# Two spectral layers of a four-layer kernel: order of the last stores and reloads, zero fills on GpSimd, and products that nobody reads

## Chip, core and metric

The kernel runs on one core of one Trainium2 chip. The metric is the device time of one execution in microseconds. The core has five engines with queues of their own: TensorE (PE in the profile, its weight loads PEld), VectorE (DVE), ScalarE (ACT), GpSimd (POOL) and SyncE (SP). SP, and here also ACT, issue the DMAs.

## What is computed

Four layers follow each other on one image of 48 x 48 tokens with 768 channels: a transformer block, a spectral layer, a scan of 12 diffusion steps, and a second spectral layer with weights of its own. Only the spectral layers are touched. Cut to what matters, one of them is:

```python
def _L3_conv_ref(x, w1, b1, w2, b2):
    xs = jnp.fft.rfft2(x, axes=(1, 2))            # 48 x 25 modes, 8 blocks of 96 channels
    xs = xs.reshape(B, H, Wm, NUM_HEADS, BLOCK)
    xr, xi = jnp.real(xs), jnp.imag(xs)
    o1r = relu(einsum(xr, w1[0]) - einsum(xi, w1[1]) + b1[0])
    o1i = relu(einsum(xi, w1[0]) + einsum(xr, w1[1]) + b1[1])
    o2r = einsum(o1r, w2[0]) - einsum(o1i, w2[1]) + b2[0]
    o2i = einsum(o1i, w2[0]) + einsum(o1r, w2[1]) + b2[1]
    out_c = softshrink(o2r, LAMBDA) + 1j * softshrink(o2i, LAMBDA)
    return jnp.fft.irfft2(out_c.reshape(B, H, Wm, C), s=(H, W), axes=(1, 2)) + x
```

## The kernel before

All values are 32-bit floats. The Fourier transforms are products with constant matrices. Along the width they are done row by row, and the half spectrum goes to two arrays in DRAM, `yu[0]` and `yu[1]`, one for each half of the channels, with 50 rows (25 modes, real and imaginary). Everything along the height is done by `spectrum_mix`, which both spectral layers call: the first under the name `f1` (from `afno_first`), the second under `f3` (from `afno_second`).

**Items.** `spectrum_mix` works on items (group of channels, chunk `kc` of 5 modes, block of 96 channels). Both layers have 40 items: `f1` has 2 groups of 4 blocks, `f3` has 4 groups of 2 blocks, and each group has 5 chunks. An item goes through four stages, and step `s` of the loop issues, in this order, the stage of four different items: `s_ifft_h` of item `s-4` (one product, and an addition to the spectrum that was loaded, L1682 and L1684), `s_mlp2` of item `s-3` (ten products, L1666 and L1667, and the shrinking, L1670 and L1672), `s_mlp1` of item `s-1` (three products, L1645 to L1647, then ACT, DVE, two ReLUs on ACT at L1655 and a sign change on POOL at L1656), and `s_fft_h` of item `s` (five products, L1631, a copy by ACT at L1633, and a sum on POOL at L1635). After each step the caller's `beside(step)` runs. The first of the three products of `s_mlp1` needs the POOL sum of its item. Steps 0 to 2 have no second layer yet, and steps 40 to 43 only empty the pipeline.

**Order.** The framework schedules each engine's instructions by priority in the order of the program, but lets one that is ready go ahead. `tc.keep_in_program_order(ins)` ties an instruction behind the one that was traced last on its engine. It ties nothing behind `ins`. DMAs of SP and ACT take eight completion semaphores in turn, in the order in which they were scheduled. A DMA first waits until the DMA that had its semaphore before has landed.

**Layer `f1`.** `afno_first` first fills the unused columns (48 to 63 of each row of 64) of three tiles with zeros on POOL: `xh`, which receives half of the layer's output, and two `homes`, which receive rows of the other half during the scan (L1754 and L1755). Then `spectrum_mix` runs over 40 items. `beside` does a few other things in between, among them the last rows of the layer's own input at steps 1 and 4. The way back along the width to `xh` begins at step 40.

**Layer `f3`.** When the last block of a chunk is through, `put` (L1865) stores the chunk to `yu` from SP (L1869). For groups 0 to 2, `put` reloads all 50 rows with six DMAs into a tile `gt` after the last chunk (L1877). For the last group (`final` = 3), the stores and reloads are tied in program order on SP, and each chunk of 10 rows is reloaded by two DMAs directly after its store. The last chunk of all is stored and reloaded in two halves, one for each block. `back(group, c)` (L1883) turns a third of the width's modes of a group back with four sets of products (L1891), copies the results out of PSUM on ACT and DVE (L64 and L66), and stores them to the output. For groups 0 to 2 these are two DMAs on ACT. For the last group they are two DMAs for every half of a third, on ACT and SP in turn. `backs` (L1900) gives the steps at which groups 0 to 2 are turned back: 8, 10 and 12 steps after the end of the group. Group 3 follows after `spectrum_mix`.

**Unread products.** `keep_warm` (L127) issues `n` products whose result nobody reads. `f3` calls it once before (L1907), with 8 products of a 96 x 96 matrix with 384 columns, between the last step and the way back of group 3. A product of 32-bit floats shows as two matmuls in the profile, so these are 16.

Of the kernel before, what the change touches and what calls it, by code (L numbers as in the profile page):

```python
# [21 lines left out]
G = 48  # L22
# [4 lines left out]
NH, HD = 12, 64  # L27
# [16 lines left out]
NB, BS = 8, 96  # L44
KW = G // 2 + 1
KC = 5
# [1547 lines left out]
def spectrum_of(yu, kc, cols):  # L1594
    return yu[2 * KC * kc : 2 * KC * (kc + 1), :, cols].rearrange("(k r) p c -> (r p) k c", r=2)


def spectrum_mix(tc, name, opened, psum, side, groups, put, beside):
# [10 lines left out]
    with tc.tile_pool(name=f"{name}_s", bufs=2, side=side) as sp:  # L1609
# [80 lines left out]
        items = [(g, kc, b) for g, (_, _, n) in enumerate(groups) for kc in range(NKC) for b in range(n)]  # L1690

        stages = {s_ifft_h: 4, s_mlp2: 3, s_mlp1: 1, s_fft_h: 0}
        for step in range(len(items) + 4):
            for stage, behind in stages.items():
                if 0 <= step - behind < len(items):
                    stage(step - behind)
            beside(step)
# [42 lines left out]
def afno_first(tc, a, yu, xh, rp, follow_in, load_next):  # L1740

    nc = tc.nc
    ev = Evac(nc)
    HC = NC // 2  # L1750
    iw = rp.tile([P, 2, G], F32, tag="iw", name="f1_iw")
    homes = [rp.tile([P, HC, 8 * HD], F32, tag=f"x2{i}", name=f"x2_{i}") for i in range(2)]
    in_rows = lambda v: v.rearrange("p c (h w) -> p c h w", w=HD)
    for v in (xh, *homes):  # L1754
        nc.gpsimd.memset(in_rows(v)[:, :, :, G:], 0.0)  # L1755
    gts = {}

    def load(half, g):
        gts[half, g] = load_spectrum(nc, rp, yu, half, g, "f1", 4)

    def back(half, g, dst, psum):
        gt = gts.pop((half, g))
        for ct in range(HC):
            ps = psum(f"w_{half}_{g}_{ct}")
            rows = ps[:, :TB].rearrange("p (j b s w) -> p j s b w", j=2, b=2, s=2)
            for i in range(4):
                nc.tensor.matmul(rows[:, i // 2, i % 2], lhsT=gt[:, i, ct * P : (ct + 1) * P], rhs=iw, start=True, stop=True)
            ev(in_rows(dst)[:, ct, :, :G], ps[:, :TB].rearrange("p (h w) -> p h w", w=G))

    with (  # L1770
        tc.tile_pool(name="f1_f", bufs=1, side="right") as fp,
        tc.tile_pool(name="f1_p", bufs=8, space=PSUM) as pm,
    ):

        def psum(tag):
            return pm.tile([P, 512], F32, tag="m", name=f"f1_{tag}")

        follow = follow_in(fp, 1)

        def first_back(g):  # L1780
            back(1, g, xh[:, :, 8 * g * HD : 8 * (g + 1) * HD], psum)
            if g + 4 < NTB:
                load(1, g + 4)

        def beside(step):
            last = 2 * NKC * (NB // 2)
            if step in (1, 4):
                follow(psum)
            elif step == 8:
                nc.sync.dma_start(iw, a["iw2"])  # L1790
                load_next()
            elif last - 12 <= step < last - 4 and step % 2 == 0:
                load(1, (step - last + 12) // 2)
            elif step >= last:
                first_back(step - last)

        with ExitStack() as stack:
            groups = [(half, 0, NB // 2) for half in (1, 0)]
            opened = spectrum_open(tc, stack, "f1", a, "L1", yu, "left", groups, 3)

            def put(group, kc, us, cols):
                nc.sync.dma_start(spectrum_of(yu[groups[group][0]], kc, cols), us[:, :, cols])

# [12 lines left out]


def afno_second(tc, a, scan, yu):

    nc = tc.nc
    ev = Evac(nc)
    out = a["out"].rearrange("(p s w) c -> s w p c", s=2, w=G)
    x3, scan_psum = next(scan)
    with ExitStack() as stack:
        GB = 2
        groups = [(n * GB // (NB // 2), n * GB % (NB // 2), GB) for n in range(NB // GB)]  # L1830
        opened = spectrum_open(tc, stack, "f3", a, "L3", yu, "right", groups, 5)
# [12 lines left out]
        for n, _ in enumerate(scan):  # L1844
            if n and n % 2 == 0:
                rows_in(n // 2 - 1, scan_psum)
            if n == 4 * NTB - 1:
                rows_in(2 * NTB - 1, scan_psum)
        bp = stack.enter_context(tc.tile_pool(name="f3_b", bufs=2, side="left"))
        pm = stack.enter_context(tc.tile_pool(name="f3_p", bufs=8, space=PSUM))  # L1850

        def psum(tag):
            return pm.tile([P, 512], F32, tag="m", name=f"f3_{tag}")

        gts = {}
        W = GB * BS
        x3p = x3.rearrange("p (j b) c -> p b j c", b=2)

        def channels(group):
            half, b0, _ = groups[group]  # L1860
            return slice(half * TB + b0 * BS, half * TB + b0 * BS + W)

        final = len(groups) - 1

        def put(group, kc, us, cols):  # L1865
            half, b0, _ = groups[group]
            cs = slice(b0 * BS + cols.start, b0 * BS + cols.stop)
            pin = tc.keep_in_program_order if group == final else lambda ins: ins
            pin(nc.sync.dma_start(spectrum_of(yu[half], kc, cs), us[:, :, cols]))  # L1869
            if kc == 0:  # L1870
                gts[group] = bp.tile([P, G // 2, W], F32, tag="gt", name=f"f3_gt_{group}")
            if group == final or kc == NKC - 1:
                rows = slice(2 * KC * kc if group == final else 0, 2 * KC * (kc + 1))
                step = G // 2 if group == final else 8
                for r0 in range(0, G // 2, step):
                    for b in range(2):
                        pin(nc.sync.dma_start(gts[group][b * HD + rows.start : b * HD + rows.stop, r0 : r0 + step, cols], yu[half][rows, b * (G // 2) + r0 : b * (G // 2) + r0 + step, cs]))  # L1877

        def store(queue, prs, cols):
            for s in range(2):  # L1880
                queue.dma_start(out[s, :, prs, cols], x3[s * HD : s * HD + G, prs, cols])

        def back(group, c):  # L1883
            cols = channels(group)
            gt = gts[group].rearrange("p (j s) c -> p s j c", s=2)
            for j in range(2):
                ps = [psum(f"w_{group}_{c}_{j}_{b}") for b in range(2)]
                for b in range(2):
                    keep = slice(b * HD, b * HD + KR)
                    for s in range(2):  # L1890
                        nc.tensor.matmul(ps[b][s * HD : (s + 1) * HD, : 2 * W], lhsT=iw[keep], rhs=gt[keep, s, 4 * c + 2 * j : 4 * c + 2 * j + 2, :], start=True, stop=True)  # L1891
                for b in range(2):
                    ev(x3p[:, b, 4 * c + 2 * j : 4 * c + 2 * j + 2, cols], ps[b][: HD + G, : 2 * W].rearrange("p (j c) -> p j c", j=2))
                if group == len(groups) - 1:
                    store((nc.scalar, nc.sync)[j], slice(8 * c + 4 * j, 8 * c + 4 * j + 4), cols)
            if group < len(groups) - 1:
                store(nc.scalar, slice(8 * c, 8 * c + 8), cols)

        each = NKC * GB
        backs = {each * (q + 1) + 8 + 2 * c: (q, c) for q in range(final) for c in range(3)}  # L1900

        def beside(step):
            if step in backs:
                back(*backs[step])

        spectrum_mix(tc, "f3", opened, psum, "left", groups, put, beside)
        keep_warm(tc, psum("warm"), opened[0][0], opened[0][1][:, :2].rearrange("p n r c -> p (n r c)"), 8)  # L1907
        for c in range(3):
            back(final, c)

# [107 lines left out]
```

## Time and profile before

| | us |
|---|---|
| time, median of 3 runs (3582.03 to 3585.97) | 3582.45 |
| time of the profiled execution | 3582.01 |
| its span, first to last instruction | 3580.2 |
| PE busy in the span (98%) | 3507.9 |
| DVE busy (56%) | 2002.3 |
| ACT busy (32%) | 1140.0 |
| POOL busy (19%) | 679.5 |
| `f1`: first `s_fft_h` of 40 items | at 2609.9 |
| `f3`: first `s_fft_h` of 40 items | at 3341.3 |
| `f3`: last addition to the spectrum starts (L1684) | at 3549.4 |
| way back of group 3 starts on PE | at 3566.5 |
| last DMA issued by SP | at 3576.0 |

The rows with "at" are places in the profiled execution, counted from the start of its span. The profiled execution takes 1.8 us more than its span, and lies 0.4 us under the median. PE's busy time counts a matmul from its start to its modelled end, at whatever clock, so 98% doesn't mean that PE did its work at full speed. The granted clock over the whole span is 0.989 of full speed.

### The profile page before, as it was taken

The page shows a single profiled execution, that of the slowest core. Times are in us where ns is not written, and L with a number is a line of the kernel's source. Part 1 is how long each engine was busy: PE and PEld are TensorE (multiplying, and loading weights), DVE is VectorE, ACT ScalarE, POOL GpSimd, SP SyncE. Part 2 cuts the span into 40 slices and gives each one's busy share as a digit, 9 for nine tenths or more (in the row PEclk, how much of TensorE's full clock was granted, in tenths as well). Part 3 has the DMA queues.
Part 4 walks back from the last instruction along what each step waited for, and adds up shares of the span by engine and source line. Part 5 has one row for each costly group of instructions (what it writes and reads, how often), then busy time and mean ns, then how long its engine had stood idle before and what let it go on. Part 6 is the DMA issues. An engine that isn't in the chain of part 4 may idle for free.

```text
span 3580.2 us, 52877 instructions
## 1 busy us (share of the span) xinstructions
PE 3507.9 (98%) x21238; PEld 2149.6 (60%) x21238; DVE 2002.3 (56%) x3015; ACT 1140.0 (32%) x1735; POOL 679.5 (19%) x566
## 2 busy tenths in 40 slices
PE   9999999999999999989999999999999998999997
PEld 5666554444444444555555555555578777996685
DVE  7644467776776776564243324232245478995454
ACT  1321255555555555103101210120023265223332
POOL 3211101111111110340000000000023303981131
PEclk9999999999999999999999999999999999999999
DMA  8555556655545443343346334534544403104356
GB/s 276 201 189 190 186 155 184 181 157 148 154 124 151 124 125 87 120 157 121 108 139 175 116 108 137 158 109 127 144 122 115 110 20 105 37 28 106 97 143 132
DMA packets 282167, 480.38 MB, mean 134 GB/s; under 512 B 39206, under 2 KB 235462, under 8 KB 275704
## 3 DMA queue, kind: packets, MB, share of 16 engines
q1 hardware_dynamic: 266568, 456.13, 43.9%
q10 hardware_dynamic: 15344, 20.75, 1.9%
q8 instruction: 171, 2.80, 0.3%
q14 instruction: 84, 0.69, 0.1%
HBM read 330.82 MB, written 145.98 MB: 133 GB/s over the span
## 4 chain that ended last, share of the span: by engine, by line
PE 90%; DVE 3%; DMA 3%; POOL 2%; ACT 1%; issue 1%; SPq 0%; ACTq 0%; POOLq 0%; DVEq 0%
PE p L996 14%; PE p L1059 13%; PE s L657 12%; PE av L688 12%; PE qk L375 6%; PE c L1223 4%; PE s L667 3%; PE c L1323 3%; PE v L180 3%; PE pj L180 2%; PE f_z L1666 2%; PE f_z L1667 2%; PE f_x L1631 2%; PE so L1410 2%; PE f_u L1682 2%; PE f_o L1645 1%
## 5 line engine op out<-in xcount | busy, mean ns | idle before, releaser
L677 DVE TENSOR_TENSOR acc<-acc,p 128x928 f32<-128x928 f32 (+1 forms) x480 | 561.1, 1169 | 258.8 <-ACT p L669 217.6
L669 ACT ACTIVATE p<-s 128x928 f32<-128x928 f32 (+1 forms) x540 | 505.9, 939 | 488.1 <-PE s L667 468.6
L657 PE MATMUL s<-qt,kv 64*128 64x464 f32 (+1 forms) x2160 | 520.8, 558 | 5.7 <-DMA qt<-q_d 5.7
L1059 PE MATMUL p<-w,h 128*128 128x384 f32 x1512 | 492.3, 487 | 0.0
L688 PE MATMUL av<-p,kv 128*64 128x464 f32 (+1 forms) x2160 | 442.6, 554 | 0.0
L1059 PEld LDWEIGHTS p<-w,h 128*128 128x128 f32 x1512 | 285.7, 190 | 198.8 <-issue 4.2
L667 PE MATMUL s<-bt,oneh 64*128 64x464 f32 (+1 forms) x1080 | 399.8, 729 | 0.8 <-DMA bt<-rh_d 0.8
L688 PEld LDWEIGHTS av<-p,kv 128*64 128x64 f32 x2160 | 147.0, 137 | 261.2 <-issue 248.8
L657 PEld LDWEIGHTS s<-qt,kv 64*128 64x128 f32 x2160 | 203.2, 187 | 162.0 <-issue 153.6
L996 PE MATMUL p<-x2nT,w 128*128 128x384 f32 x864 | 292.8, 489 | 4.2 <-POOL rr L1035 4.2
L1323 PE MATMUL c<-H,bands 128*48 128x96 f32 x5632 | 244.6, 247 | 10.9 <-DVE th L1261 8.3
L375 PE MATMUL qk<-xnT,wqk 128*128 128x384 f32 x756 | 249.8, 487 | 0.1
L1323 PEld LDWEIGHTS c<-H,bands 128*48 128x48 f32 x5632 | 234.8, 123 | 20.9 <-issue 8.7
L996 PEld LDWEIGHTS p<-x2nT,w 128*128 128x128 f32 x864 | 164.8, 191 | 120.8 <-POOL rr L1035 4.4
L996 PE MATMUL p<-xT,w 128*128 128x384 f32 x648 | 220.8, 486 | 0.0
L1035 POOL TENSOR_TENSOR rr<-rr,ml_b 128x1152 f32<-128x1152 f32 x12 | 31.8, 2649 | 944.7 <-DMA rr<-xr_d 828.3
L991 ACT ACTIVATE h<-h,ml_b 128x384 f32<-128x384 f32 x144 | 88.3, 614 | 345.8 <-DVE h L1011 173.6
L375 PEld LDWEIGHTS qk<-xnT,wqk 128*128 128x128 f32 x756 | 141.5, 190 | 93.1 <-issue 0.7
L1331 POOL TENSOR_TENSOR t<-s,c 128x768 f32<-128x768 f32 x80 | 144.4, 1828 | 180.8 <-DVE s L1294 168.2
L996 PEld LDWEIGHTS p<-xT,w 128*128 128x128 f32 x648 | 123.2, 190 | 85.8
L667 PEld LDWEIGHTS s<-bt,oneh 64*128 64x128 f32 x1080 | 106.8, 187 | 105.4 <-issue 103.3
L1666 PE MATMUL f_z<-f_w,f_o 97*96 97x96 f32 x800 | 134.2, 249 | 0.0
(334 smaller groups left out, 4594.0 us busy)
## 6 DMA issues: line engine op xcount, KB each, us to landing
w<-w1s_d SPq DMA_DIRECT2D x36, 768.0 KB
w<-w2s_d SPq DMA_DIRECT2D x36, 768.0 KB
w<-w1s_d SPq DMA_DIRECT2D x36, 576.0 KB
w<-in_mlp_w_dram SPq DMA_DIRECT2D x27, 768.0 KB
yu<-f_ys SPq DMA_DIRECT2D x48, 384.0 KB
wqk<-wqk_d SPq DMA_DIRECT2D x12, 1344.0 KB
bt<-rw_d SPq DMA_DIRECT2D x72, 174.0 KB
bt<-rh_d SPq DMA_DIRECT2D x72, 174.0 KB
```

Of the source, the lines that this page charges most:

```text
L180: nc.tensor.matmul(p[:, :TB], lhsT=rhs[n][:, c, t * P : (t + 1) * P], rhs=w[:, c, :], start=c == 0, stop=c == NC2 - 1)
L375: nc.tensor.matmul(p[:, :TB], lhsT=w[:, n, c, :], rhs=ops[sb][n][:, c, :], start=c == 0, stop=c == NC2 - 1)
L657: nc.tensor.matmul(ps[:, s, :n], lhsT=keys[pr % 2][rows, kt * P : (kt + 1) * P], rhs=held(c)[rows, :n], start=True, stop=False)
L667: nc.tensor.matmul(ps[:, s, :n], lhsT=oneh[rows, b % 2, :], rhs=bts[b // 2][rows, j, :n], start=False, stop=True)
L669: nc.scalar.activation(p, ps[:, :, :n], AF.Exp)
L677: nc.vector.tensor_tensor(probs[c], probs[c], p, ALU.add)
L688: nc.tensor.matmul(avs[c][rows, : size(c)], lhsT=vals[pr % 2][:, kt, rows], rhs=p[:, s, :], start=kt == 0, stop=kt == NT - 1)
L996: nc.tensor.matmul(p[:, :TB], lhsT=w[n][:, c, :], rhs=rhs[n][:, c, :], start=c == 0, stop=c == NC2 - 1)
L1059: nc.tensor.matmul(ps[t][:, :TB], lhsT=hs[left, f][:, t * P : (t + 1) * P], rhs=wt[:, f % KW2, :], start=f == 0, stop=f == NF2 - 1)
L1323: nc.tensor.matmul(ps[r0 : r0 + G, k // 4, cols], lhsT=bands[:, n - GC, i, :] if gr else bands0[:, n, i, :], rhs=H[:, n, :, d : d + NPR], ...
L1331: GP.tensor_tensor(t, sc[:, ch], c1[:, m0 : m0 + GC].unsqueeze(2).to_broadcast([P, GC, RR, NPR]), ALU.mult)
L1666: nc.tensor.matmul(out, lhsT=o1[:, j, 1:3, :].rearrange("c r h -> c (r h)"), rhs=w2t[:, b, 0, :], start=True, stop=False)
```

## The change

`spectrum_mix` gets seven unread products: three before step 0, two at the start of step 1 and two at the start of step 2. They use a PSUM tile of their own, the first that the loop takes. Both layers get them.

In `f1` the three zero fills at the start are gone. Nine smaller ones, each for a third of a tile (one of three channel tiles), are issued at the end of steps 9 to 17, each tied behind what POOL was given before it.

In `f3` the last chunk is stored as a whole. The chunk before it (`kc` 3) is stored without its reload, so that the order on SP is: store of chunk 3, store of chunk 4, two reloads of chunk 3, the first reload of chunk 4. The second reload of chunk 4 is issued by ACT. The three parts of the way back of group 2 are issued at steps 38, 39 and 40, where they were at 38, 40 and 42. The unread products at the end become 12, from 8.

```diff
         stages = {s_ifft_h: 4, s_mlp2: 3, s_mlp1: 1, s_fft_h: 0}
+        warm = psum("first")
+        unread = lambda n: keep_warm(tc, warm, fh, w1t[:, :2].rearrange("p n r c -> p (n r c)"), n)
+        unread(3)
         for step in range(len(items) + 4):
+            if 0 < step < 3:
+                unread(2)
             for stage, behind in stages.items():
...
-    for v in (xh, *homes):
-        nc.gpsimd.memset(in_rows(v)[:, :, :, G:], 0.0)
+    edges = [in_rows(v)[:, ct, :, G:] for v in (xh, *homes) for ct in range(HC)]
...
         def beside(step):
             last = 2 * NKC * (NB // 2)
+            if 8 < step < 9 + len(edges):
+                tc.keep_in_program_order(nc.gpsimd.memset(edges[step - 9], 0.0))
...
         def put(group, kc, us, cols):
             half, b0, _ = groups[group]
-            cs = slice(b0 * BS + cols.start, b0 * BS + cols.stop)
+            if cols.stop < W:
+                return
+            cs = slice(b0 * BS, b0 * BS + W)
             pin = tc.keep_in_program_order if group == final else lambda ins: ins
-            pin(nc.sync.dma_start(spectrum_of(yu[half], kc, cs), us[:, :, cols]))
+            pin(nc.sync.dma_start(spectrum_of(yu[half], kc, cs), us))
             if kc == 0:
                 gts[group] = bp.tile([P, G // 2, W], F32, tag="gt", name=f"f3_gt_{group}")
-            if group == final or kc == NKC - 1:
-                rows = slice(2 * KC * kc if group == final else 0, 2 * KC * (kc + 1))
-                step = G // 2 if group == final else 8
-                for r0 in range(0, G // 2, step):
+
+            def reload(queue, b, rows, r0, n):
+                pin(queue.dma_start(gts[group][b * HD + rows.start : b * HD + rows.stop, r0 : r0 + n], yu[half][rows, b * (G // 2) + r0 : b * (G // 2) + r0 + n, cs]))
+
+            chunk = lambda k: slice(2 * KC * k, 2 * KC * (k + 1))
+            if group < final and kc == NKC - 1:
+                for r0 in range(0, G // 2, 8):
                     for b in range(2):
-                        pin(nc.sync.dma_start(gts[group][...], yu[half][rows, ..., cs]))
+                        reload(nc.sync, b, slice(0, KR), r0, 8)
+            elif group == final and kc != NKC - 2:
+                for k in (kc,) if kc < NKC - 1 else (kc - 1, kc):
+                    for b in range(2):
+                        reload(nc.scalar if k == NKC - 1 and b else nc.sync, b, chunk(k), 0, G // 2)
...
-        backs = {each * (q + 1) + 8 + 2 * c: (q, c) for q in range(final) for c in range(3)}
+        backs = {each * (q + 1) + 8 + (2 if q < final - 1 else 1) * c: (q, c) for q in range(final) for c in range(3)}
...
-        keep_warm(tc, psum("warm"), opened[0][0], opened[0][1][:, :2].rearrange("p n r c -> p (n r c)"), 8)
+        keep_warm(tc, psum("warm"), opened[0][0], opened[0][1][:, :2].rearrange("p n r c -> p (n r c)"), 12)
```

More of the change, by code (lines that the diff above doesn't have):

```diff
@@ L1866, in put @@
             half, b0, _ = groups[group]
-            cs = slice(b0 * BS + cols.start, b0 * BS + cols.stop)
+            if cols.stop < W:
+                return
+            cs = slice(b0 * BS, b0 * BS + W)
             pin = tc.keep_in_program_order if group == final else lambda ins: ins
-            pin(nc.sync.dma_start(spectrum_of(yu[half], kc, cs), us[:, :, cols]))
+            pin(nc.sync.dma_start(spectrum_of(yu[half], kc, cs), us))
             if kc == 0:
                 gts[group] = bp.tile([P, G // 2, W], F32, tag="gt", name=f"f3_gt_{group}")
-            if group == final or kc == NKC - 1:
-                rows = slice(2 * KC * kc if group == final else 0, 2 * KC * (kc + 1))
-                step = G // 2 if group == final else 8
-                for r0 in range(0, G // 2, step):
-                    for b in range(2):
-                        pin(nc.sync.dma_start(gts[group][b * HD + rows.start : b * HD + rows.stop, r0 : r0 + step, cols], yu[half][rows, b * (G // 2) + r0 : b * (G // 2) + r0 + step, cs]))
+            def reload(queue, b, rows, r0, n):
[3 more added lines that the diff above has]
+                for r0 in range(0, G // 2, 8):
+                    for b in range(2):
+                        reload(nc.sync, b, slice(0, KR), r0, 8)
[3 more added lines that the diff above has]
+                        reload(nc.scalar if k == NKC - 1 and b else nc.sync, b, chunk(k), 0, G // 2)
         def store(queue, prs, cols):
```

## The prediction

> **What bounds the kernel now.** The page gives PE 98% busy and 90% of the chain of waits, so the question is where PE works slowly or stands still in the two spectral layers. I cut the stretches that the change touches out of the busy times by window (columns: length, busy time and instructions of each engine, granted PE clock, DMA share, GB/s):
>
> ```profile
> 2609.90:2626.90 17.00, 11.36 (x61) 9.58 (x62) 3.25 (x9) 4.13 (x9) 6.33 (x8) 0.60 0.99 271
> 3341.20:3356.40 15.20, 12.25 (x62) 10.48 (x63) 2.60 (x7) 4.13 (x9) 3.63 (x5) 0.55 0.21 52
> 3356.40:3370.00 13.60, 13.60 (x115) 11.45 (x114) 7.86 (x15) 5.03 (x12) 4.39 (x6) 1.00 0.21 55
> 3548.00:3566.50 18.50, 6.27 (x22) 2.86 (x19) 2.08 (x5) 0.48 (x1) 0.00 (x0) 0.75 0.59 112
> ```
>
> The first two rows are the first items of `f1` and `f3`: PE has gaps and only 0.55 to 0.60 of its clock. The third row is the running pipeline, PE full at full clock. The fourth is the end of `f3`, where little runs.
>
> The timeline shows the POOL part of the first stretch:
>
> ```profile
> 2616.72 0.81 POOL L1656 TENSOR_SCALAR f_o<-f_o 96x240 f32<-96x240 f32 x1 [4.34 <-ACT f_o L1655]
> 2617.48 2.01 POOL L1755 MEMSET xh<- 128x2304 f32 x1
> 2619.43 0.78 POOL L1755 MEMSET x<- 128x384 f32 x2
> 2620.18 0.69 POOL L1635 TENSOR_TENSOR f_Xs<-f_X 96x240 f32<-96x240 f32 x1
> 2620.92 0.39 PEld L1645 LDWEIGHTS f_o<-f_Xs,f_w 96*96 96x96 f32 x2 [4.41 <-POOL f_Xs L1635]
> ```
>
> The fills stand between the sign change of item 0 and the sum of item 1, whose copy had ended at 2617.34. PE waits 4.41 us for that sum.
>
> The SP part of the timeline, for the end of `f3`:
>
> ```profile
> 3547.45 0.31 SPq L1869 DMA_DIRECT2D yu<-f_us  x1
> 3550.40 1.24 SPq L1877 DMA_DIRECT2D f_gt<-yu  x2
> 3552.82 0.45 SPq L1869 DMA_DIRECT2D yu<-f_us  x1
> 3558.19 0.69 SPq L1877 DMA_DIRECT2D f_gt<-yu  x2
> 3558.98 0.31 SPq L1869 DMA_DIRECT2D yu<-f_us  x1
> 3563.11 0.69 SPq L1877 DMA_DIRECT2D f_gt<-yu  x2
> 3566.53 6.68 PE L1891 MATMUL f_w<-f_gt,iw 50*64 50x384 f32 x48 [12.19 <-DMA f_gt<-yu]
> ```
>
> Store and reload take turns: chunk 3, then the two halves of chunk 4. Each reload waits for its store to land, and the next store stands behind it on SP. The last data exist at 3550.08 (second L1684 at 3549.43, 0.65 us), and PE starts at 3566.53. Finally SP's waits:
>
> ```profile
> SPq L1869 <- DMA out_dram<-x: 9.4, 3, 6.3
> ```
>
> Stores to `yu` also wait for output DMAs of `back` of group 2 (issued by ACT at 3540.73 and 3549.02), which had their semaphores before them.
>
> **What the Trainium skill says.** (1) "TensorE: Matmul & The Clock Gate", Part 1: PE's clock falls to half after an idle window of about 3.4 us and comes back after a busy one; the window runs freely. The trace agrees: after gaps of 1.8 and 1.5 us the pair of L1646 takes 1.01 us (2613.34) where it takes 0.57 at full clock (3356.87), and full speed is back some 13 us later. (2) "DMA: Bandwidth & Descriptors", "Two DMAs through the same engine are not ordered": a DMA that reads what another wrote must wait for that one's completion. That is the 2.95 us (3547.45 to 3550.40) to 5.4 us of each store above. (3) Same page, "Issuing engines are not separate DMA queues": a second issuing engine only saves issue time. Two reloads on SP take 0.69 us, so ACT saves about 0.35.
>
> **The change, part by part.** The profiled execution took 3582.0 us (span 3580.2), 0.4 under the median.
>
> *First items, pace.* From one item's first-layer weight load to the next's, before: `f3` 3343.78, 3349.52, 3356.38, that is 5.7 and 6.9 us; `f1` 2612.43, 2620.92, 2626.91, that is 8.5 and 6.0. At full clock, from the load at 3356.38 the next item's sum ends at 3360.82; with 0.06 for PE to react the shortest pace is 4.5. The steady pace is 4.57.
>
> *Do the unread products hold the clock?* A call is two matmuls at a spacing of 0.323 us (3549.02 to 3549.34 and on), so 0.645. Two calls, 1.29, fill the gap of 1.45 before the first `s_mlp1` (PE gap at 2612.44 and 3343.78); in step 2 they leave about 1 us of the gap idle. I take it that the clock stays at 1.00. Then both layers need 2.51 (first `s_fft_h` to first `s_mlp1`, as before) + 4.5 + 4.5 = 11.5 us to the third `s_mlp1`, after which PE is full.
>
> *The three at the start.* In `f3`, PE starts at 3341.27, just after DVE had emptied the last PSUM tile of the scan at 3341.17. The unread tile is now the first of its pool and I take it to wait for the same, so 3 x 0.645 = 1.9 us come on top. In `f1` PE is free at 2608.07, the last PSUM tile is emptied at 2608.67 (2606.82 + 1.85), and the spectrum lands for PE's start at 2609.9. So three calls end at 2610.65: +0.8. If they wait for PE alone the cost is nothing (gains 0.8 and, in `f3`, 1.8 more); at half clock it is twice.
>
> *Fills.* They cost 2.0 and 0.42 us for 2304 and 384 columns, which makes 0.10 + 0.83 ns per column: a third costs 0.74 or 0.2. In a running step POOL is idle 3.1 us after its sum (its wait before L1656 at full pace), and the tie puts each fill there. Zero; were it before the sum instead, at most 3 x 0.74.
>
> *Sum of both starts.* `f1`: before 2626.91 - 2609.89 = 17.0; after 0.8 + 11.5; gain 4.7. `f3`: before 3356.38 - 3341.24 = 15.1; after 1.9 + 11.5; gain 1.7. Behind `f1` everything waits for its results, so the gain passes through.
>
> *Way back of group 2 moved.* It takes 1.52 us of PE (16 matmuls). Step 39 and step 40 are full, step 42 waits for DVE. One part leaves step 42, where it cost little, and comes into step 39: the last addition ends at 3551.3 instead of 3550.1 (+1.4 for PE, -0.2 as DVE copies less before it). In return all four output DMAs are issued by about 3542.5 and land (6.7 us at worst, 3540.73 to 3547.45) before the last store: the waits for semaphores vanish.
>
> *Last chunk.* Store 3 goes out when its data are there, about 3543.5. Store 4 follows at 3551.4 with nothing before it. Landing: 2.95 as for store 3, which is as large; 3.2 taken, up to 5.4 beside other traffic. Reloads of chunk 3 are issued meanwhile. Reloads of chunk 4 go out at 3554.6. They took 3.4 until PE started (3563.11 to 3566.53), for half the width; twice the bytes, 0.35 less issue: 3.7 (3.1 to 4.6). PE starts at 3558.3: gain 8.2. The reload on ACT waits for store 4; behind it on ACT stand only the copies of group 3, which need it anyway.
>
> *End.* 12 unread calls from 3550.3 take 7.74 us, to 3558.0, just before PE is wanted; if the reload is faster they delay it, by 0.3 at most. PE then starts at full clock: 48 matmuls in 4.6 (3 x 1.52) and not 6.68. The first output DMA left 2.9 us after PE's start and would leave 1.2 earlier; the DMA rate at the end (up to 275 GB/s for 1.77 MB) limits the rest. Gain 2.0 (0.5 to 3).
>
> Sum: 4.7 + 1.7 + 8.2 + 2.0 = 16.6 us. 3582.0 - 16.6 = 3565.4; with the 0.4 of the median, 3565.9.
>
> **Rivals.** About 0.2%, 7 us, is what a measurement can tell from no change.
> - *The clock falls anyway.* Unread calls at half clock take 2.6 instead of 1.29 and delay the items: `f1` -2.7 (fills) + 0.8 + 1.1 + 1.2 = +0.4, `f3` 1.9 + 1.1 + 1.2 = +4.2, end -8.2: 3.6 less, 3578.8. For it: windows with a 1.5 us gap lost the clock before. Against: the gaps are mostly filled now.
> - *The end pays less.* Store 4 takes 5.4, reloads 4.6, and the outputs stay bound by DMA: the end gives 4.9 in place of 10.2; 3571.2.
> - *A gain of `f1` is lost in the scan*, whose loads of bands and angles stand in the chain with 9.71 and 7.85 us: if they end no earlier, 3570.6. Against: their room is freed only after `f1`.
> - *Slower.* The four output DMAs of steps 39 and 40 now follow each other on ACT. If each of three had to wait for a semaphore whose DMA had just gone out, at 6.6 us (3540.73 to 3547.4), ACT would hold the last two items' ReLUs back 19.8 us: 3582.4 - 16.6 + 19.8 = 3585.6. It decides from 16.6 us on. Against: before, ACT's output pairs went out in 0.85 to 0.92 us, and its waits for semaphores ahead of them were 1.3 us at most.
>
> **Numbers.** Forecast 0.60; end pays less 0.15; lost in the scan 0.12; clock falls 0.09; slower 0.04. Faster by over 0.2%: 0.87; within: 0.09; slower: 0.04. The lower end of the range takes starts without PSUM waits (-2.6) and an end better by 1.9 (the lower bounds above); the upper end takes in both cases around 3571, with 4 us more for their coming partly together, and leaves out the last two: 3561 to 3575.
>
> **What would show it.** Right: clock near 1.00 in the first 12 us of both layers; pace 4.5 from item 0 on; no fill between sign change and sum; store 4 under 0.2 us after the last addition; PE's way back starting 7 us after that addition ends, where it was 16.4; its 48 matmuls in under 5 us. Wrong: a clock near 0.6 with the unread matmuls spaced 0.64; a store that waits for an output DMA; ACT standing still in steps 40 to 42.

## The result, and where the time went

| | before | changed |
|---|---|---|
| time, median of 17 runs each, us | 3585.97 | 3575.55 |
| lowest and highest | 3580.32, 3588.72 | 3573.19, 3579.94 |
| profiled execution: time, span | 3582.0, 3580.2 | 3578.7, 3576.8 |

The ratio is 0.9976, with a 95% interval of 0.9969 to 0.9982: by it the change gains 8.6 us (6.5 to 11), where 16.6 had been forecast; the medians themselves differ by 10.4. The forecast's 3565.9 was counted from the first three runs of the kernel before (3582.45), its range ended at 3575, and the changed kernel's median is 3575.55. The direction was right, the size was not.

The two profiled executions can't be compared by their spans. PE ends the MLP ahead of `f1`, before any changed instruction, at 2608.07 before and at 2614.49 in the changed kernel. In the twelve experiments, whose instructions up to there are the changed kernel's, that place lies between 2606.91 and 2613.80, so it scatters by itself. I therefore cut both executions at the same places of the program and compare the stretches:

| stretch, us | before | changed | gain | forecast |
|---|---|---|---|---|
| end of the MLP to the third first-layer load of `f1` (PEld L1645) | 18.84 | 14.22 | 4.6 | 4.7 |
| from there to `f3`'s first work on PE (rest of `f1`, scan) | 714.36 | 712.53 | 1.8 | 0 |
| from there to the third first-layer load of `f3` | 15.11 | 13.42 | 1.7 | 1.7 |
| from there to the first part of group 2's way back | 171.97 | 171.96 | 0.0 | 0 |
| from there to the end of the last addition | 21.73 | 24.75 | -3.0 | -1.2 |
| from there to the start of group 3's way back | 16.45 | 11.88 | 4.6 | 9.4 |
| from there to the end of the span | 13.67 | 13.55 | 0.1 | 2.0 |
| sum | 972.1 | 962.3 | 9.8 | 16.6 |

Both starts came out as forecast, and the three last rows did not. The busy times by window of the changed kernel (columns: length, busy time and instructions of PE, PEld, DVE, ACT, POOL, granted clock, DMA share, GB/s), for the first items of `f1` and of `f3`, and for the time between the last addition and the way back:

```profile
2617.20:2628.70 11.50, 9.93 (x71) 7.34 (x69) 2.79 (x8) 3.92 (x9) 3.62 (x5) 1.00 1.05 259
3343.20:3354.70 11.50, 9.97 (x72) 7.38 (x70) 1.91 (x5) 3.92 (x9) 3.62 (x5) 1.00 0.19 51
3551.40:3563.20 11.80, 7.02 (x22) 3.26 (x20) 0.00 (x0) 0.00 (x0) 0.00 (x0) 0.93 0.62 94
```

The clock of the first items is 1.00 where it was 0.60 and 0.55, and both take the 11.5 us that the forecast's steps gave. The timeline of `f1` shows the sum right behind the sign change, with no fill between them, and a load 4.5 us after the one before (2619.69):

```profile
2622.72 0.81 POOL L1656 TENSOR_SCALAR f_o<-f_o 96x240 f32<-96x240 f32 x1 [3.08 <-ACT f_o L1655]
2623.49 0.69 POOL L1635 TENSOR_TENSOR f_Xs<-f_X 96x240 f32<-96x240 f32 x1
2624.23 0.24 PEld L1645 LDWEIGHTS f_o<-f_Xs,f_w 96*96 96x96 f32 x2 [1.59 <-POOL f_Xs L1635]
```

The end of `f3` in the timeline of the changed kernel (start, duration, engine, line; PE, DVE and the two queues that issue DMAs):

```profile
3543.88 1.25 PE L1682 MATMUL f_u<-f_Z,f_ih 96*96 96x480 f32 x2 [1.53 <-DVE f_Z L1672]
3544.92 0.53 PE L1666 MATMUL f_z<-f_w,f_o 97*96 97x96 f32 x2
3545.24 0.53 PE L1667 MATMUL f_z<-f_w,f_o 97*96 97x96 f32 x2
...
3550.72 0.65 DVE L1684 TENSOR_TENSOR f_us<-f_u,f_yt 96x480 f32<-96x480 f32 x1 [0.58 <-PE f_u L1682]
3551.40 0.31 SPq L1877 DMA_DIRECT2D yu<-f_us  x1
3551.80 3.59 SPq L1882 DMA_DIRECT2D f_gt<-yu  x3
3555.17 0.56 ACTq L1882 DMA_DIRECT2D f_gt<-yu  x1
3563.25 6.98 PE L1906 MATMUL f_w<-f_gt,iw 50*64 50x384 f32 x48 [4.83 <-DMA f_gt<-yu]
```

Store 4 leaves SP 0.03 us after the last addition (3550.72 + 0.65 = 3551.37): the queue is free, as forecast. The two reloads of chunk 3 follow it at once, and those of chunk 4 go out 3.7 us later, when it has landed (the row of three on SP holds both of chunk 3 and the first of chunk 4, the row on ACT the second). That is also near the forecast. But PE then waits until 3563.25, 8.1 us after the issue of chunk 4's reload, where 3.7 had been forecast. In addition the ten products of the last item (L1666, L1667) run at a spacing of 0.32 us between the lines, half the pace of 0.17 at full clock, and so does the way back at the end: 6.98 us for its 48 matmuls, not 4.6.

What the DMAs did meanwhile is seen in two windows of the same kernel, first the wait for group 3's reloads, then the reloads of group 0, whose pieces are as long (192 numbers, 768 bytes) but which take 50 rows at once:

```profile
3555.00:3562.00 7.00, 3.42 (x11) 1.47 (x9) 0.00 (x0) 0.00 (x0) 0.00 (x0) 0.97 0.72 81
3405.00:3409.00 4.00, 4.00 (x34) 3.28 (x33) 2.62 (x5) 1.68 (x4) 1.08 (x2) 1.00 0.69 183
```

The last column is the point: 81 GB/s against 183, at about the same share of busy time of the DMA engines. 7 us at 81 GB/s are 567 KB, which is what was left of the 737 KB of the reloads of chunks 3 and 4 when store 4 had landed.

### The profile page after: what moved, and what is told of

The parts are those of the page before. It is cut to its first block, busy times and chain, and to the rows that moved or that the text cites. A ratio compares the mean times of both kernels' runs of the same rounds, so it can differ in the third digit from the quotient of the medians.

```text
span 3576.8 us, 52953 instructions
## 1 busy us (share of the span) xinstructions
PE 3513.7 (98%) x21274; PEld 2148.0 (60%) x21274; DVE 2004.7 (56%) x3015; ACT 1141.4 (32%) x1735; POOL 680.8 (19%) x572
## 4 chain that ended last, share of the span: by engine, by line
PE 91%; DVE 3%; POOL 2%; DMA 2%; ACT 1%; issue 1%; SPq 0%; ACTq 0%; DVEq 0%; POOLq 0%
PE p L996 14%; PE p L1059 13%; PE s L657 12%; PE av L688 12%; PE qk L375 6%; PE c L1223 4%; PE s L667 3%; PE c L1323 3%; PE v L180 3%; PE pj L180 3%; PE f_u L1682 2%; PE f_z L1666 2%; PE f_z L1667 2%; PE so L1410 2%; PE f_x L1631 2%; POOL t L1331 1%
## 5 line engine op out<-in xcount | busy, mean ns | idle before, releaser
L1666 PE MATMUL f_z<-f_w,f_o 97*96 97x96 f32 x800 | 134.1, 249 | 0.0
```

Source lines behind the costliest of these rows:

```text
L1666: nc.tensor.matmul(out, lhsT=o1[:, j, 1:3, :].rearrange("c r h -> c (r h)"), rhs=w2t[:, b, 0, :], start=True, stop=False)
```

## The experiments

One execution of a kernel scatters by several us, so the single times below decide nothing. The stretches do. Columns: (a) end of the MLP to the third first-layer load of `f1`, (b) `f3`'s first work on PE to its third such load, (c) first part of group 2's way back to the end of the last addition, (d) from there to the start of group 3's way back, (e) its 48 matmuls, (f) its start to the end of the span.

| kernel | a | b | c | d | e | f | one time |
|---|---|---|---|---|---|---|---|
| before | 18.84 | 15.11 | 21.73 | 16.45 | 6.68 | 13.67 | 3582.01 |
| changed | 14.22 | 13.42 | 24.75 | 11.88 | 6.98 | 13.55 | 3578.66 |
| e1_reload3_first | 14.22 | 14.66 | 23.14 | 12.89 | 6.68 | 13.60 | 3574.19 |
| e2_one_queue | 14.22 | 15.07 | 25.03 | 11.11 | 5.52 | 13.72 | 3578.86 |
| e3_backs_apart | 14.21 | 14.91 | 23.37 | 12.75 | 7.82 | 13.54 | 3573.77 |
| e4_warm_19 | 14.22 | 14.70 | 23.14 | 11.50 | 4.72 | 12.77 | 3576.48 |
| e5_no_first_unread | 16.33 | 15.07 | 24.94 | 11.67 | 4.98 | 13.54 | 3576.93 |
| e6_fills_at_start | 16.21 | 15.08 | 25.25 | 12.02 | 6.69 | 13.40 | 3574.85 |
| e7_gap_filled | 14.21 | 15.08 | 23.14 | 12.21 | 7.84 | 13.25 | 3570.96 |
| e8_all_three | 14.21 | 13.41 | 23.14 | 13.93 | 6.85 | 13.30 | 3575.23 |
| e9_long_pieces | 14.21 | 14.66 | 23.14 | 10.40 | 8.32 | 14.65 | 3576.86 |
| e10_twenty_rows | 14.22 | 14.72 | 23.14 | 8.31 | 4.52 | 13.01 | 3571.99 |
| e11_thirds | 14.22 | 14.88 | 23.14 | 11.54 | 6.00 | 11.83 | 3571.01 |
| e12_rows_and_gap | 14.21 | 14.74 | 23.14 | 8.65 | 6.28 | 12.48 | 3569.30 |

All edits are to the changed kernel.

### The two starts: fills and unread products

`e5_no_first_unread` takes the seven unread products and their tile away:

```diff
-        unread(3)
...
-            if 0 < step < 3:
-                unread(2)
```

> The changed kernel without the seven unread products at the first items of both layers. Theory (they hold the clock): without them the clock is 0.6 again in the first 15 us; from the end of the last matmul of the layer before to the third item's first-layer weight load, f1 takes 16.2 us (18.8 before, less 2.7 for the fills; 14.2 with the change), and f3 15.1 from its first matmul (13.5 with the change). Rival (in f1 the fills alone were it): f1 14.2 to 14.7.

`e6_fills_at_start` puts the fills back:

```diff
+    for v in (xh, *homes):
+        nc.gpsimd.memset(in_rows(v)[:, :, :, G:], 0.0)
...
-            if 8 < step < 9 + len(edges):
-                tc.keep_in_program_order(nc.gpsimd.memset(edges[step - 9], 0.0))
```

> The changed kernel with the three zero fills at the start of f1 again. Theory: they stand between the sign change of item 0 and the sum of item 1 and cost about 2.7 us, 16.9 us from the last matmul before f1 to the third item's first-layer weight load (14.2 with the change). With a longer gap the clock may fall too: up to 18. Rival (POOL has room for them beside the unread products): 14.2 to 14.5.

The first three first-layer products of `f1` in the timeline, first of `e5_no_first_unread`, then of `e6_fills_at_start`:

```profile
2615.72 1.11 PE L1645 MATMUL f_o<-f_Xs,f_w 96*96 96x240 f32 x2 [1.45 <-POOL f_Xs L1635]
2621.52 1.12 PE L1645 MATMUL f_o<-f_Xs,f_w 96*96 96x240 f32 x2 [1.48 <-POOL f_Xs L1635]
2627.30 0.61 PE L1645 MATMUL f_o<-f_Xs,f_w 96*96 96x240 f32 x2
```

```profile
2613.55 0.65 PE L1645 MATMUL f_o<-f_Xs,f_w 96*96 96x240 f32 x2 [0.16 <-POOL f_Xs L1635]
2619.03 0.92 PE L1645 MATMUL f_o<-f_Xs,f_w 96*96 96x240 f32 x2 [1.88 <-POOL f_Xs L1635]
2624.57 0.65 PE L1645 MATMUL f_o<-f_Xs,f_w 96*96 96x240 f32 x2
```

Without the unread products the pair takes 1.11 us (half clock) and the pace is 5.8. With them, but with the fills, the pair starts at 0.65 and the second waits 1.88 us for a sum that the fills delay. Alone, the moved fills gain 2.5 us (18.84 to 16.33) and the unread products 2.6; together 4.6. The clock of the first 14.1 us is 0.64 in e5, near the 0.6 expected; e6 came out 0.7 us better than expected. The forecast's steps for `f1` hold, and its gain is the same 14.2 in every kernel that has both. It isn't lost later: measured from the end of the MLP, the first product of the way back to `xh` starts at 191.5 us before and at 186.6 in the changed kernel.

`f3` is another matter. Twelve kernels have the unread products there, and only the changed kernel and `e8_all_three` show the gain of 1.7 us. The other ten lie between 14.66 and 15.08, against 15.07 to 15.11 without them. The three calls of the start, in the changed kernel and then in `e7_gap_filled`, where nothing differs up to there:

```profile
3341.24 2.15 PE L133 MATMUL f_first<-f_w,f_fh 96*96 96x384 f32 x6 [1.78 <-issue]
```

```profile
3333.56 3.50 PE L133 MATMUL f_first<-f_w,f_fh 96*96 96x384 f32 x6 [1.78 <-issue]
```

PE has stood idle for 1.78 us in both. The calls come behind this wait and can't fill it. In one kernel the clock holds, in the other it has fallen, and the calls that should keep it cost 1.4 us more. The forecast's 1.7 was met by this profile's luck; what the luck is made of is told below, with the last item. The median of the twelve is 14.7, a gain of 0.4.

### The last item: the clock and the moved way back

`e3_backs_apart` puts group 2's parts back to steps 38, 40 and 42; `e7_gap_filled` fills PE's gaps in the last two steps:

```diff
-... (2 if q < final - 1 else 1) * c: (q, c) ...
+... 2 * c: (q, c) ...
```

> The changed kernel with the way back of group 2 at steps 38, 40 and 42 again. Theory (the moved parts delay the last items, by PE time and by a fallen clock): from PE's start of the first part of group 2's way back to the end of the last addition 21.7 us, as in the kernel before, where the changed kernel has 24.7; clock 1.00 there. Against it stands what the move was to save: then the outputs of step 42 meet the last store, and from the last addition to PE's way back it takes 12.5 to 16 us instead of 11.9. Rival (nothing but the outputs matters): 24.7 us stay.

```diff
             if 0 < step < 3:
                 unread(2)
+            if name == "f3" and step > len(items) + 1:
+                keep_warm(tc, psum(f"late_{step}"), fh, w1t[:, :2].rearrange("p n r c -> p (n r c)"), 2)
```

> The changed kernel with two unread products ahead of each of the last two items' products of s_ifft_h in f3 (steps 42 and 43), where PE waits 1.4 to 1.5 us for DVE. Theory (the clock falls in that gap and the ten products of the last item's second layer take 3.3 instead of 1.7 us): from PE's first part of group 2's way back to the end of the last addition 23.1 us instead of 24.7. Rival (the moved parts cost this time by themselves): 24.4 to 25.

Column c answers. With the way back moved it is 23.14 wherever the clock held, which is the forecast's own number (21.73 + 1.4, where 1.2 had been taken). It is 24.75 to 25.25 where the clock fell in the last item. Without the filled gaps it fell in four of nine (changed, e2, e5, e6) and held in five (e1, e4, e9, e10, e11). With them it held in all three (e7, e8, e12), as the busy times of e7 from c's start to its end say (clock in the third column from the end):

```profile
3520.60:3543.80 23.20, 22.83 (x172) 14.48 (x172) 12.98 (x24) 6.55 (x16) 3.77 (x5) 1.00 0.70 147
```

Which of the two happens goes by where PE's wait falls. In all fourteen traces the granted clock changes only at places that lie multiples of 3.413 us apart: in the changed kernel at 3544.52, 3547.94, 3561.59, 3568.42 and 3571.83, which is 1, 4, 2 and 1 times that. The series lies elsewhere in each execution. In the last items PE waits once for 1.53 us (3542.35 to 3543.88 in the changed kernel) and once for 1.43. In the four executions whose clock fell, the wait of 1.53 us lies whole between two neighbouring places of the series, and the clock falls at the second; in the five where it held, one of the places lies inside it. The changed kernel, first between the places around its wait and then up to the next one:

```profile
3541.11:3544.52 3.41, 1.88 (x17) 1.48 (x16) 1.54 (x3) 0.00 (x0) 0.74 (x1) 1.00 0.89 132
3544.52:3547.93 3.41, 3.41 (x20) 3.01 (x19) 0.00 (x0) 0.00 (x0) 0.00 (x0) 0.50 0.91 215
```

In `e10_twenty_rows` the wait is from 3541.47 to 3543.00, a place of its series is at 3541.91, and the clock is held from there on:

```profile
3541.93:3545.33 3.40, 2.33 (x20) 1.88 (x21) 0.89 (x2) 0.00 (x0) 0.00 (x0) 1.00 0.97 195
```

With the calls of e7 there is no such wait, as PE isn't idle for 0.3 us at a time in this stretch, and so three out of three is more than luck. The start of `f3` goes by the same series. In the changed kernel and in `e8_all_three` a place lies inside the wait of 1.79 us and leaves 1.52 and 1.36 us of it behind; in the twelve other executions, that of before and e5 among them, 1.64 us or more lie between two places, and the clock fell in each.

In `e3_backs_apart` the clock fell too, from 3538.11 to 3541.53: one product took 1.73 us instead of 1.05, most of the ten products behind it ran at half pace, and c became 23.37 rather than 21.7. Its d is 12.75, since store 4 now shares the queues with the last output DMAs and takes 5.7 us. At full clock it would have needed 21.7 + 12.75 = 34.5 us for c and d, and the changed kernel 23.14 + 11.88 = 35.0. So moving the way back gains nothing that these runs can show.

### The reloads

`e2_one_queue` issues the last reload from SP:

```diff
-reload(nc.scalar if k == NKC - 1 and b else nc.sync, b, chunk(k), 0, G // 2)
+reload(nc.sync, b, chunk(k), 0, G // 2)
```

> The changed kernel with all reloads issued by SP. Backlog theory: the queue doesn't matter but for 0.35 us of issue, 11.9 to 12.3 us from the last addition's end to PE's way back. Rival (two queues get in each other's way): below 11 us.

PE began after 11.1 us, but with four matmuls only. It then waited for the second half of the data, with the next ones at 3564.81, which is 12.5 us after the addition. So the second queue isn't dear, and not worth much: 0.6 us (12.5 against 11.9).

My first theory for the 8.1 us was that chunk 3's reload stands ahead of chunk 4's. `e1_reload3_first` sends it before store 4:

```diff
-            elif group == final and kc != NKC - 2:
-                for k in (kc,) if kc < NKC - 1 else (kc - 1, kc):
+            elif group == final:
+                for k in (kc,):
```

> The changed kernel with chunk 3 reloaded directly after its store again, so ahead of the store of chunk 4; the rest as changed. Changed kernel: 11.9 us from the end of the last addition to PE's way back of group 3. Backlog theory (reloads move at some 80 GB/s, and after the store 737 KB of four reloads stand in line): only 368 KB are left, so 0.1 + 3.6 (store) + 4.6 (368 KB at 80 GB/s) + 1.2 (landing to PE) = 9.5 us. Rival (the reload of chunk 4 is slow by its width or by its two queues, whatever stands before it): 11.5 to 12 us.

It became worse, 12.89. SP's queue in the timeline of that kernel:

```profile
3537.55 0.31 SPq L1877 DMA_DIRECT2D yu<-f_us  x1
3545.60 0.69 SPq L1882 DMA_DIRECT2D f_gt<-yu  x2
3546.39 0.31 SPq L1877 DMA_DIRECT2D yu<-f_us  x1
3553.25 0.27 SPq L1882 DMA_DIRECT2D f_gt<-yu  x1
```

Store 3 needed 8.05 us until its reload could go: the DMA engines were full there, at shares of 1.00 to 1.12 from 3539 to 3543, with the outputs of group 2 under way. Store 4 was then ready at 3545.91 and left at 3546.39, side by side with the reload, and took 6.9 us where it takes 3.7 in the changed kernel. And with nothing else left, chunk 4's reload alone still took 5.5 us from issue to PE. So the order is not the cause. The theory fell, and the question became why ten rows take so long.

`e9_long_pieces` gives group 3 a DRAM array of its own, `e10_twenty_rows` reloads both chunks at once, `e11_thirds` cuts each reload in three:

```diff
+    yu.append(dram.tile([HD, G, 2 * BS], F32, tag="yz", name="yz"))
...
-            cs = slice(b0 * BS, b0 * BS + W)
+            cs = slice(0, W) if group == final else slice(b0 * BS, b0 * BS + W)
+            half = 2 if group == final else half
```

> Group 3's spectrum goes through a DRAM array of its own, [rows, 48, 192], so that a row of a reload is one run of 18432 bytes; in the changed kernel it is 24 pieces of 768 bytes that lie 1536 bytes apart. Bytes, queues and order are as in the changed kernel. There, 551 KB that were left of the reloads when store 4 had landed moved at 58 to 98 GB/s and took 7 us, and the way back began 11.9 us after the last addition. Theory 1, the 768-byte pieces set that rate: long pieces move at 160 GB/s or more, as the reloads of groups 0 to 2 do (162 to 210 GB/s at 3405 to 3409), the 551 KB take 3.5 us, and the way back begins 8.4 us after the last addition (8 to 9). Rival, the ten rows (ten partitions) of a reload set it: the rate stays near 80 GB/s and the 11.9 stay, within 0.5.

```diff
-                for k in (kc,) if kc < NKC - 1 else (kc - 1, kc):
-                    for b in range(2):
-                        reload(nc.scalar if k == NKC - 1 and b else nc.sync, b, chunk(k), 0, G // 2)
+                rows = chunk(kc) if kc < NKC - 1 else slice(2 * KC * (kc - 1), 2 * KC * (kc + 1))
+                for b in range(2):
+                    reload(nc.scalar if kc == NKC - 1 and b else nc.sync, b, rows, 0, G // 2)
```

> The reloads of chunks 3 and 4 are one: two DMAs of twenty rows, both behind store 4, in place of four of ten rows, two of them ahead of its landing. Pieces stay at 768 bytes, the bytes are the same. Theory 1, the pieces set the rate of 80 GB/s: 737 KB start only at about 3.1 us after the last addition, and need 9 us: the way back begins 13 us after the last addition (12.5 to 14). Rival, the rows set it (groups 0 to 2 reload fifty rows at once, in pieces of 768 bytes, at 162 to 210 GB/s): twice the rate with twenty rows, 4.6 us for the bytes and 1.3 until the first and after the last: 9.0 us (8.5 to 10).

```diff
-                        reload(..., b, chunk(k), 0, G // 2)
+                        for r0 in range(0, G // 2, 8):
+                            reload(..., b, chunk(k), r0, 8)
```

> Each reload of ten rows is cut into three of 8 pieces a row, as the reloads of groups 0 to 2 are cut: 12 DMAs in place of 4, same bytes, same pieces, same order and queues. Theory 1 (pieces) and the rival (rows) expect the rate of 80 GB/s and a way back 11.9 us after the last addition, up to 1 us later for six more issues on SP of 0.3 us. A third theory, that the rate is set by how many DMAs are under way at once (groups 0 to 2 have six): 120 GB/s or more, and a way back 10 us after the last addition or less.

Windows of four us that hold the reload behind the landing of store 4, first of `e1_reload3_first` (ten rows in pieces of 768 bytes, one DMA on SP and one on ACT), then of `e9_long_pieces` (ten rows in runs of 18432 bytes), then of `e10_twenty_rows` (twenty rows in pieces of 768 bytes, one DMA on SP and one on ACT):

```profile
3554.00:3558.00 4.00, 0.00 (x0) 0.00 (x0) 0.00 (x0) 0.00 (x0) 0.00 (x0) 0.80 0.53 92
```

```profile
3555.00:3559.00 4.00, 2.00 (x7) 0.72 (x5) 0.00 (x0) 0.00 (x0) 0.00 (x0) 1.00 0.69 92
```

```profile
3553.00:3557.00 4.00, 2.94 (x10) 1.18 (x8) 0.00 (x0) 0.00 (x0) 0.00 (x0) 1.00 0.56 181
```

With long pieces chunk 4's reload moves no faster. The 92 GB/s of its window say too much, because a packet is counted where it starts, and these packets of 18432 bytes take 2.2 us each: from the first start to the last end the reload took 5.4 us, 68 GB/s, where that of e1 took 4.1 us, 91 GB/s. d was 10.40 all the same, 1.5 us less than in the changed kernel and between the two expectations, which is not explained. But the clock then fell and f grew, so d and f together are only 0.4 us shorter (25.05 against 25.43). Twice the rows in as many DMAs (e10) move twice the bytes in the same time, 4.1 us from the first start to the last end. In thirds (e11) the rate was 82 GB/s from 3549 to 3557. So the pieces' length and the number of DMAs under way are not what limits, and the rows per DMA are. The timeline of `e10_twenty_rows`:

```profile
3548.91 0.31 SPq L1877 DMA_DIRECT2D yu<-f_us  x1
3551.88 0.28 SPq L1882 DMA_DIRECT2D f_gt<-yu  x1
3551.89 0.60 ACTq L1882 DMA_DIRECT2D f_gt<-yu  x1
3557.19 4.52 PE L1906 MATMUL f_w<-f_gt,iw 50*64 50x384 f32 x48 [1.25 <-DMA f_gt<-yu]
```

The store lands in 2.97 us with nothing beside it, the reload takes 5.3, and PE starts 8.3 us after the last addition, although no reload runs beside the store any more. It starts at full clock, because the 12 calls now end only 1.25 us ahead of it.

Why the rows count stays open. The Trainium skill ("DMA: Bandwidth & Descriptors", "Why a DMA increments its semaphore by 16 and not by 1") says that such a copy is split over the largest number of engines up to 16 that divides the slowest dimension of both sides. That is ten for ten rows and for twenty alike. The packets on record agree: each of these DMAs ends with ten packets of 4 bytes, in e1 as in e10. So the number of engines doesn't tell the two apart. What differs is the time of one packet of 768 bytes, in the mean 60 and 80 ns on the two queues with ten rows, 41 and 37 with twenty. A limit that lies with the rows, as each goes to one partition of SBUF, would fit: 92 GB/s over twenty rows under way and 181 over forty are both about 4.6 GB/s. The 78 GB/s of e2 (3556 to 3563), with all reloads on one queue, don't fit this simplest form, and no run tried such a limit by itself.

### The end

`e4_warm_19` issues 19 unread calls at the end in place of 12, so that they reach PE's start:

> The changed kernel with 19 unread products at the end instead of 12, so that they reach to within 0.5 us of the reload's landing. Theory (the clock had fallen by the way back): its 48 matmuls take 4.6 us instead of 6.98, and from their start to the end of the span 11.5 us instead of 13.6. Rival (the end is bound by the issue and landing of the output DMAs): the matmuls take 4.6, the end moves by less than 0.5 us, 13.1 or more.

The clock held and the 48 matmuls took 4.72 us, but the end came only 0.8 us nearer: 12.77, between the two expectations. The busy times from the first output DMA's issue until the data have flowed, in the changed kernel and then in `e4_warm_19`:

```profile
3566.20:3575.00 8.80, 4.02 (x34) 1.62 (x26) 2.79 (x5) 2.20 (x5) 0.00 (x0) 0.69 0.79 200
```

```profile
3564.10:3573.00 8.90, 2.55 (x28) 1.06 (x20) 2.79 (x5) 2.10 (x5) 0.00 (x0) 0.88 0.80 198
```

The outputs' 1.77 MB take the same time at 200 GB/s. A faster PE only lets the first of them go earlier, 2.2 us after its start rather than 2.9, and that difference is the gain. Column f says the same over all kernels: with 4.5 to 5.0 us for the matmuls it is 12.8 to 13.5, with 6.0 and more 11.8 to 14.7.

### Together

`e8_all_three` joined e1, e7 and 15 calls at the end, on the strength of the first theory:

> Three edits at once on the changed kernel: chunk 3 reloaded ahead of the last store, unread products ahead of the last two items' s_ifft_h, 15 unread products at the end. If each does what its theory says: 23.1 us to the last addition, 9.5 us from there to PE's way back (the 15 calls end at 9.7, so about 9.8), 4.6 us for its matmuls and 11.5 to 12 from its start to the end of the span; f3 ends 1.6 + 2.1 + 1.8 = 5.5 us earlier than with the change. If the output DMAs bind the end, 3.7.

c is the 23.14 expected, but d is 13.93: store 4 left 1.6 us after the last addition, behind chunk 3's reload, and landed 6.9 us later. It shows the cost of e1's order a second time. `e12_rows_and_gap` joins the edits of e10 and e7 instead and was timed:

> The edits of e10_twenty_rows (one reload of twenty rows for chunks 3 and 4) and of e7_gap_filled (two unread calls in each of the last two steps) together. If the rows set the rate of the reloads and the unread calls keep the clock in the last item: from the first part of group 2's way back to the last addition 23.1 us (in the changed kernel 24.75), from there to the way back of group 3 8.3 us (8 to 9; changed 11.9), 48 matmuls in 4.5 us, start to end of the span 13.0. That is 5.7 us less than the changed kernel's profile, or 3570 by its median: 0.9958 of the kernel before (0.9950 to 0.9966). Rival, what the end gains is lost in the output DMAs, which cannot move faster: start to end of the span 15 us or more, ratio 0.9970 or more.

Its median of 5 runs is 3570.63 (3567.97 to 3571.89) beside 3584.16 for 9 runs of the kernel before; the ratio is 0.9959, with an interval of 0.9945 to 0.9973. c is 23.14 and d 8.65. The median lies 5 us under that of the changed kernel (3575.55), close to the 5.7 that the stretches gave. The two intervals overlap, so the order of these two kernels rests on the stretches more than on the times. The clock fell again, 1.4 us after the start of the way back (6.28 for the matmuls), and f was 12.48 all the same.

## Why the forecast was wrong, by its steps

**Right.** *First items, pace; the fills; the three at the start of `f1`*: 14.22 us where 18.84 - 4.7 = 14.1 was forecast, with clock 1.00 and pace 4.5, and each half of it confirmed alone (e5, e6). *Behind `f1` the gain passes through*: it does. *Store 4 with nothing before it* left after 0.03 us. *No wait of a store for an output DMA*, and no stall of ACT in steps 40 to 42. *Way back of group 2 moved*: the cost of 1.2 was 1.4 at full clock.

**Wrong: the term "twice the bytes, 0.35 less issue: 3.7" of the last chunk.** It measured 8.1. The row used was for half the width, 3.4 us for 184 KB a half, and the step took the time as nearly independent of the bytes. The window that the forecast itself drew (3548.0 to 3566.5) had only a mean rate. Cut into small windows, the same trace shows the half-width reload moving at 92 GB/s:

```profile
3564.00:3566.00 2.00, 0.00 (x0) 0.00 (x0) 0.00 (x0) 0.00 (x0) 0.00 (x0) 0.50 0.52 92
```

With that, 3.4 plus 184 KB at 92 GB/s (2.0 us) is 5.4 for chunk 4, which is what e1 measured (5.5). The rest is the reload of chunk 3, "issued meanwhile": it was issued, but at this rate it needs 4 us itself and was less than half done when store 4 landed (567 of 737 KB were left). Both together are the 4.4 us. This step alone costs more than half of the missing 8.

**Wrong: "PE then starts at full clock" and the 2.0 at its end.** The calls ended at 3558.4, 4.8 us ahead of the late reload, and the clock fell: 6.98 us, gain 0.1. Had it held, e4 shows that it pays 0.8, because the output DMAs set the rest. The lower bound of 0.5 was nearer than the value taken.

**Wrong by chance: the clock in the last item, -1.6.** I had taken full clock there. It held in five of nine executions without filled gaps and fell in this one, as its wait of 1.53 us lay whole between two places of the series. The forecast had no term for this, although it had seen the clock fall after gaps of 1.8 and 1.5 us itself.

**Met by chance.** `f3`'s start paid its 1.7 here, but typically pays 0.4. The 1.8 of the scan isn't the change's either: with the same instructions, the stretch from `f1`'s third load to `f3` is 710.7 to 714.5 us over the experiments. In the trace of before the clock fell early in the scan (0.76 of full speed from 2823 to 2830), and in the changed kernel it held at the same place. But it fell there in five experiments too, with stretches of 711.8 to 714.5 us, and held in seven, with 710.7 to 712.7, so that this is a part of the scatter at most.

Of the rivals, "the end pays less" names what happened, for a reason of its own: it had 5.4 for the store and 4.6 for the reload, and it was 3.7 and 8.1. (Its 4.9 us for the end come to 5.1 with the 3.2 and 3.7 that the forecast had taken.) "The clock falls anyway" was right for the last item, the end and mostly for `f3`, and wrong for `f1`. Put in order, what the change is worth by the stretches, without the luck, is 4.6 in `f1`, 0.4 in `f3`, -1.4 to -3.0 in the last item, 4.6 in the wait and 0.1 at the end: 6.7 to 8.3, beside the measured 8.6.

## What to carry to other kernels

When a transfer stands alone on the path, read its rate in a window of a few us around it, and scale by bytes and by rows; a mean over a stage with other traffic says nothing, and a time from issue to landing hides which part grows. Before a transfer is sent earlier, ask what it then runs beside: chunk 3's reload sent ahead of store 4 made the store twice as long, and one reload of twenty rows behind it was better than two of ten, one of them early. Where a wait of 1.5 us can cost the clock, count on it falling in some executions, fill the wait itself, since products behind it come too late, and compare stretches of several runs, not one profile.

## What the hardware showed that I had not expected

- A reload of ten rows moved at 68 to 92 GB/s (before, changed, e1, e2, e9, e11), in pieces of 384, 768 or 18432 bytes, on one queue or two, whole or in thirds. Reloads of twenty rows moved at 181 GB/s (e10), those of fifty at 183.
- PE's clock changed only at places that are multiples of 3.413 us apart, and whether it fell depended on where PE's wait lay between them. The Trainium skill ("TensorE: Matmul & The Clock Gate", Part 1) says that the window of about 3.4 us runs freely and that the clock is therefore run-variable, which agrees. But its table of the two states speaks of an idle window, and the forecast was wrong to read its own trace, with gaps of 1.8 and 1.5 us, as agreeing with that. Here a wait of 1.53 us that lay whole between two neighbouring places was enough four times out of four in the last items, with PE at work on both sides of it, while 1.52 us left the clock up once at the start of `f3`. Waits of 1.43 us that lay whole between two places in the last items lost it twice (e3, e11) and left it up five times.
- A store of 369 KB landed in 3.0 us alone (e10), in 3.7 with a reload issued behind it, and in 6.9 with a reload issued ahead of it (e1, e8).
